# A cross-attention and mixture-of-experts kernel: routing two tiles earlier, first expert tables inside the attention loop, left scatters in threes

## The chip, the cores and the metric

The kernel runs on one NeuronCore of a Trainium2 chip. The metric is the device time of one execution in microseconds (us). Work is split over five engines that run their own instruction streams and meet at semaphores: PE (TensorE: matmuls and transposes; PEld is its weight load), DVE (VectorE), ACT (ScalarE), POOL (GpSimd, which also issues the row scatters) and SP (SyncE, which issues most other transfers).

## The reference, cut to what matters

Input is x of 4 sequences x 1024 tokens x 256, and a context of 77 rows per sequence. All is float32.

```
h   = layernorm(x)
s   = (h Wq + bq)(ctx Wk + bk)^T            # 16 heads of 64, 77 keys each
o   = softmax(s) (ctx Wv + bv) Wo + bo
x1  = x + gamma * norm(h + o) + beta        # norm: layernorm over 256, eps 1e-3
f   = layernorm(x1)
p   = softmax(f Wg)                         # 32 experts
w, i = top_k(p, 4)
y   = sum over k of  w[k] * swiglu(f; W1[i[k]], W3[i[k]], W2[i[k]])     # H = 128
z   = swiglu(f; Ws1, Ws3, Ws2)              # shared FFN, H = 256
out = x1 + y + z
```

Each expert takes at most CAP (2048) pairs of a token and an expert. With 4096 tokens and four experts each, there are 16384 pairs, which is 128 full tiles of 128 rows and some more for the unfilled ends.

## The kernel before

The tokens are cut into 8 blocks of 512 (`NB`), and each block into 4 tiles of 128 tokens (`NC`), so that there are 32 tiles `t`; `blk` is t // 4 and `c` is t % 4. y is block 6 and z is block 7. A block's rows live in `y0[blk]` all through.

**Preparation** multiplies the weights into per-sequence matrices `mq` (scores straight from h) and `vo` (output straight from the probabilities).

**The attention loop** runs over the 32 tiles. In a tile: three groups of heads (6, 5, 5) of `scores` on PE, each with its row maximum `mx` on DVE (L438); `soften`, 16 exponentials on ACT with their sums (L446); `invert`, the reciprocal of the sums on DVE (L456); `divide`, three multiplications on POOL (L461). One tile later PE turns the probabilities (`turn_p`, L479), DVE copies the first part of the result and ACT the rest (L484, L487, L488), PE makes `po` (`output`, L497), and DVE adds it and takes its mean and variance (`residual`, L505 and L355, L356).

Around this, the loop carries steps of other blocks, chosen by `c`:

- for the next block: `measure_in` (DVE statistics), `scale_in` (POOL), `norm_in` (a DVE shift, then four ACT passes, L365), `turn_in` (PE, two ACT copies, L412), `bias_in` (POOL), `keep` (DVE, y = x + beta, L403, in four pieces);
- for block `ffn` = blk - 1: `measure_out` (POOL), `settle` (DVE: two operations L523 and L526, then statistics, in four pieces), `measure_ffn` (POOL), `norm_ffn` (a DVE shift, four ACT passes);
- for block `old` = blk - 2: `turn_ffn` (PE, two ACT copies, L553), `gate` (PE), `turn_gate` (an ACT copy and a PE transpose), `chances` (DVE), `powers` (ACT), `choose` (DVE, top 4 and weights), `mark` (DVE, one-hot of the choices and running counts, L619, L626, L630), `count` (PE), `place` (DVE and POOL, the row number of each pair), and `send`: 16 scatters of 128 rows each, one indirect transfer on POOL's queue (L674), which write each token's row into the buffer `xr` in DRAM, sorted by expert.

**The bridge** follows: it ends block z's normalisation, routes y and z, runs the shared FFN of y and z (`shared_in`, `shared_mid`, `shared_out`: PE ph L704 and pz L730, ACT sg L713, DVE hT), and makes the tables "a": for the first 64 expert tiles, which rows of `xr` they read and which expert they belong to. They come from the counts of blocks 0 to 5. It also issues the last expert weights on SP.

**The expert loop** runs over tiles `j`, four steps deep. SP fetches eight tiles at a time (g, 8 x 136 KB, through row numbers in registers); PE turns g (pgT, copied to gT by DVE, L1080), makes peh (L1086), turns h, makes py (L1107); DVE scales it (L1111); POOL scatters the result rows to `ys` (L1112). Scatters to `xr` that are still open when the loop starts, called left here, are sent one per three tiles; tables "z" for the other tiles are made in its first steps. A switch runs as many of the remaining tiles as the counts ask for.

**The tail** gathers four result rows per token, adds them, and runs the shared FFN of blocks 1 to 5 beside it.

All four are written inside `as_written()`, which pins the order of the instructions on each engine to the order of the code. The order on an engine is thus read directly from the order of the calls.

Of the kernel before, what the change touches and what calls it, by code (L numbers as in the profile page):

```python
# [16 lines left out]
P = 128  # L17
NE = 32
# [12 lines left out]
def kernel(  # L31
# [73 lines left out]
    iota_j = const.tile([P, NJ], F32, name="iota_j")  # L105
    nc.gpsimd.iota(iota_j, [[1, NJ]], base=0, channel_multiplier=0, allow_small_or_imprecise_dtypes=True)
# [260 lines left out]
    def means(name):  # L367
        return sm.tile([P, NC, 2], F32, tag="mv", name=f"mv_{name}", bufs=6)
# [300 lines left out]
    def send(blk, i0, i1):  # L669

        row, xn = rows[blk], xns[blk]
        for i in range(i0, i1):
# [12 lines left out]
            if blk < BA:  # L685
                early.append(sct.ins)
            else:

                tc.declare_no_dep(sct.ins, group="firsts", reason="distinct rows")
                tc.add_to_no_dep_group("lates", sct.ins)  # L690

# [56 lines left out]
    measure_in(0)  # L748
    scale_in(0)
    norm_in(0)  # L750
    turn_in(0)
    bias_in(0)
    keep(0, 0, NC)
    xts[1] = load(1)
    with as_written():
        for t in range(NT):
            blk, c = t // NC, t % NC
            ffn, old = blk - 1, blk - 2
            ahead = blk + 1 < NB
            if c == 0 and blk + 2 < NB:  # L760
                xts[blk + 2] = load(blk + 2)
            if t == 0:

                nc.sync.dma_start(xr[NE * PLACES :, :], none)
                nc.sync.dma_start(
                    xr[: NE * PLACES, :].rearrange("(e q) r -> q e r", q=PLACES)[:P],
                    none.unsqueeze(1).to_broadcast([P, NE, ROW]),
                )
            if t == 18:
                nc.sync.dma_start(ws13[:, :, 0, :], Ws1.rearrange("(k p) f -> p k f", p=P))  # L770
                nc.sync.dma_start(ws13[:, :, 1, :], Ws3.rearrange("(k p) f -> p k f", p=P))
                nc.sync.dma_start(ws2, Ws2.rearrange("(k p) f -> p k f", p=P))
            if t in parts:
                load_experts(*parts[t])
            if c == 1 and ahead:
                scale_in(blk + 1)
            if c == 1 and ffn >= 0:
                measure_out(ffn, 2, 4)
            if c == 3 and ahead:
                bias_in(blk + 1)  # L780
            if c == 3:
                measure_out(blk, 0, 2)
            if c == 3 and ffn >= 0:
                measure_ffn(ffn)
            if c == 1 and old >= 0:
                gate(old)
            if c == 3 and old >= 0:
                count(old)
            sv = [scores(t, g) for g in range(2)]
            if c == 1 and old >= 0:  # L790
                turn_gate(old)
                chances(old)
            soften(t, 0, sv[0])
            if c == 1 and old >= 0:
                powers(old)
            soften(t, 1, sv[1])
            sv.append(scores(t, 2))
            if t >= 1:
                for i in range(3):
                    turn_p(t - 1, i)  # L800
            soften(t, 2, sv[2])
            if c == 0 and old >= 0:
                turn_ffn(old)
            if c == 2 and ahead:
                turn_in(blk + 1)
            if c == 0 and ahead:
                measure_in(blk + 1)
            if c == 1 and old >= 0:
                choose(old)
            if c == 2 and old >= 0:  # L810
                mark(old)
            if c == 3 and old >= 0:
                place(old)
# [496 lines left out]
```

## Time and profile before

| what | us |
|---|---|
| median of 3 runs (lowest, highest) | 800.23 (798.41, 801.84) |
| the profiled execution | 800.8 |
| its span in the profile | 799.0 |
| attention loop, to the end of the last po | 401.25 |
| first peh of the expert loop | 449.30 |
| start of the gather and the tail, about | 732 |

The granted TensorE clock of the profiled execution was 0.974 in the mean. Over the span PE was busy for 733.9 us (92%), DVE for 527.1 (66%), POOL for 402.9 (50%) and ACT for 334.1 (42%). A row of a timeline or a group gives the engine, the line of the code, the operation and its tiles, then its time; a bracket behind it gives the idle time before it and what ended that. In a chain of waits, "issue" is time in which the engine waited for nothing that the profile shows.

### The profile page before, as it was taken

To read this page: it belongs to the slowest core of one execution; us is meant where nothing else is said; L and a number is where in the kernel's file an instruction comes from. 1 tells how busy PE (TensorE), PEld (TensorE's weight loads), DVE (VectorE), ACT (ScalarE), POOL (GpSimd) and SP (SyncE) were. 2 spreads that over 40 slices of the span, in tenths; PEclk is the share of its full clock that TensorE was granted. 3 is DMA by queue.
4 is the path that set the end of the run, shared out by engine and by line. 5 is a ranking of instruction groups with operands and counts; after the bars stand their busy time and mean duration, and the time that the engine had idled before them with its cause. 6 is when DMAs were issued, how large, how long until landed. Compare 5 with 4: busy or idle time off the path is not lost.

```text
span 799.0 us, 12911 instructions
## 1 busy us (share of the span) xinstructions
PE 733.9 (92%) x3508; PEld 542.2 (68%) x3508; DVE 527.1 (66%) x1455; ACT 334.1 (42%) x1586; POOL 402.9 (50%) x488
## 2 busy tenths in 40 slices
PE   6999999999999999999968578879999999999796
PEld 4775767777777777776735457667888878776454
DVE  1874565778777787767665355545767666473897
ACT  0647667676666677766521112221222222221000
POOL 2003333347777777777886355555555555443000
PEclk9999999999999999999998889999999999999988
DMA  8930000404135221513175244465555545422996
GB/s 269 333 101 1 1 1 1 132 1 141 58 100 185 80 98 57 162 57 115 57 242 169 75 125 136 138 197 165 189 165 162 182 146 160 149 96 90 412 412 246
DMA packets 78867, 111.97 MB, mean 140 GB/s; under 512 B 9995, under 2 KB 63679, under 8 KB 78783
## 3 DMA queue, kind: packets, MB, share of 16 engines
q1 hardware_dynamic: 59519, 66.14, 26.7%
q0 software_dynamic: 13056, 36.72, 12.7%
q10 hardware_dynamic: 6208, 8.17, 2.9%
q8 instruction: 31, 0.51, 0.3%
q14 instruction: 53, 0.43, 0.2%
HBM read 62.36 MB, written 48.64 MB: 139 GB/s over the span
## 4 chain that ended last, share of the span: by engine, by line
PE 72%; DVE 10%; ACT 6%; issue 4%; DMA 4%; POOL 3%; DVEq 0%; ACTq 0%; SPq 0%; POOLq 0%
PE peh L1086 16%; PE po L497 14%; PE sc L430 13%; PE py L1107 7%; ACT p L446 5%; PE pgT L1078 4%; PE ph L704 3%; PE pz L730 3%; PE pp L479 2%; PE phT L1100 2%; PE pvo L262 1%; POOL xr L674 1%; PE pvo L287 1%; PE pm L262 1%; DMA gy<-ys 1%
## 5 line engine op out<-in xcount | busy, mean ns | idle before, releaser
L1112 POOL DMA_INDIRECT ys<-y,place x144 | 138.0, 959 | 130.0 <-DVE y L1111 81.2
L446 ACT ACTIVATE p<-sc,mx 128x77 f32<-128x77 f32 x512 | 159.1, 350 | 93.2 <-DVE mx L438 93.2
L1086 PE MATMUL peh<-we,gT 128*128 x576 | 155.0, 393 | 17.7 <-issue 11.4
L497 PE MATMUL po<-we,pT 128*128 128x256 f32 (+1 forms) x640 | 147.1, 383 | 4.6 <-DVE pT L484 3.3
L674 POOL DMA_INDIRECT xr<-xn,row x128 | 127.6, 997 | 35.6 <-issue 34.6
L461 POOL TENSOR_TENSOR p<-p,su 128x385 f32<-128x385 f32 (+1 forms) x96 | 91.0, 973 | 97.2 <-DVE su L456 76.3
L430 PE MATMUL sc<-we,qT 128*128 128x385 f32 (+1 forms) x384 | 138.9, 509 | 0.9 <-POOL qT L416 0.9
L497 PEld LDWEIGHTS po<-we,pT 128*128 128x128 f32 (+1 forms) x640 | 118.4, 190 | 26.7 <-DVE pT L484 5.4
L1094 ACT ACTIVATE h<-peh 128x128 f32<-128x128 f32 x144 | 40.1, 278 | 217.2 <-PE peh L1086 143.8
L1086 PEld LDWEIGHTS peh<-we,gT 128*128 128x128 f32 x576 | 101.5, 196 | 29.7 <-issue 12.8
L446 ACT ACTIVATION_READ_ACCUMULATOR p<-sc,mx 128x1 f32 x512 | 118.7, 232 | 0.0
L430 PEld LDWEIGHTS sc<-we,qT 128*128 128x128 f32 x384 | 71.1, 189 | 54.3 <-issue 27.7
L1095 DVE TENSOR_TENSOR h<-peh,h 128x128 f32<-128x128 f32 x144 | 41.8, 291 | 84.6 <-ACT h L1094 69.1
L1107 PE MATMUL py<-we,ehT 128*128 x288 | 88.3, 389 | 0.9 <-ACT ehT L1102 0.8
L1111 DVE TENSOR_SCALAR y<-py,own 128x256 f32<-128x256 f32 x144 | 69.5, 483 | 17.2 <-PE py L1107 13.1
L438 DVE TENSOR_REDUCE mx<-sc 128x5 f32<-128x385 f32 (+1 forms) x96 | 54.3, 576 | 33.8 <-PE sc L430 31.3
L1080 DVE COPY gT<-pgT 128x256 f32<-128x256 f32 x144 | 59.8, 415 | 7.4 <-PE pgT L1078 4.8
L1078 PE MATMUL pgT<-ident,g 128*128 128x128 f32 x288 | 55.9, 278 | 1.1 <-issue 0.4
L1107 PEld LDWEIGHTS py<-we,ehT 128*128 128x128 f32 x288 | 44.5, 195 | 12.6 <-ACT ehT L1102 1.7
L1078 PEld LDWEIGHTS pgT<-ident,g 128*128 128x128 f32 x288 | 40.6, 144 | 16.9 <-issue 1.6
L1100 PE MATMUL phT<-ident,h 128*128 128x128 f32 x144 | 40.2, 279 | 8.2 <-DVE h L1095 5.9
L730 PE MATMUL pz<-ws,hT 128*128 128x256 f32 x128 | 35.5, 431 | 11.8 <-DVE hT L719 6.3
(200 smaller groups left out, 927.4 us busy)
## 6 DMA issues: line engine op xcount, KB each, us to landing
g<-xr SPq DMA_DIRECT2D x144, 136.0 KB
gy<-ys SPq DMA_DIRECT2D x16, 1024.0 KB
xr<-y SPq DMA_DIRECT2D x1, 4352.0 KB
y<-in_x SPq DMA_DIRECT2D x8, 512.0 KB
out<-y ACTq DMA_DIRECT2D x16, 256.0 KB
xnd<-xnT SPq DMA_DIRECT2D x6, 512.0 KB
we<-in_W SPq DMA_DIRECT2D x8, 384.0 KB
ys<-y,place POOLq DMA_INDIRECT x144
```

What stands on the lines that cost most here:

```text
L430: nc.tensor.matmul(sc[:, : (h1 - h0) * SK], qTs[blk][:, k, o : o + P], mq[:, b, k, h0 * SK : h1 * SK], start=(k == 0), stop=(k == KC - 1),)
L446: nc.scalar.activation(probs[t][:, h, :], sv[:, h - h0, :], AF.Exp, bias=mx[:, h : h + 1], accum_out=su[:, h : h + 1],)
L461: nc.gpsimd.tensor_tensor(p[:, h0:h1, :], p[:, h0:h1, :], su[:, h0:h1].unsqueeze(2).to_broadcast([P, h1 - h0, SK]), ALU.mult,)
L497: nc.tensor.matmul(po[:, :D], pT[:n, i, :], vo[b][:n, i, :], start=(i == 0), stop=(i == KT - 1))
L674: sct = nc.gpsimd.indirect_dma_start(out=xr, out_offset=bass.IndirectOffsetOnAxis(ap=row[:, i : i + 1], axis=0), in_=xn[:, c, :], in_offse ...
L730: nc.tensor.matmul(pz[:, c * D : (c + 1) * D], hT[:, f, (2 * c2 + c) * P : (2 * c2 + c + 1) * P], ws2[:, f, :], start=(f == 0), stop=(f == ...
L1078: nc.tensor.transpose(pt[:, k * P : (k + 1) * P], g[:, j % RG, k * P : (k + 1) * P], ident)
L1080: nc.vector.tensor_copy(gT.rearrange("p k t -> p (k t)"), pt[:, :D])
L1086: nc.tensor.matmul(ph[:, : 2 * H], gT[:, k, :], we[:, ds(ev[j] * EW + k * 2 * H, 2 * H)], start=(k == 0), stop=(k == KC - 1),)
L1107: nc.tensor.matmul(py[:, :D], hT, we[:, ds(ev[j] * EW + KC * 2 * H, D)], start=True, stop=True)
L1111: nc.vector.tensor_scalar(y, py[:, :D], own[:, i, 1:2], None, ALU.mult)
L1112: sent = nc.gpsimd.indirect_dma_start(out=ys, out_offset=bass.IndirectOffsetOnAxis(ap=place_[:, i : i + 1], axis=0), in_=y, in_offset=None,)
```

## The change

The order of the loop's side steps is rewritten; nearly nothing is added or removed.

- `measure_in` of block blk + 2 is called at c = 2; `scale_in` and `norm_in` of the next block at c = 0, `turn_in` at c = 1, `bias_in` at c = 2 (each one tile earlier than before, from block 1 on).
- For `ffn`: the three pieces of `settle` that were called at c = 0, 1 and 2 are called together at c = 1, behind `invert` and `divide`. `measure_ffn` and `norm_ffn` come at c = 2, `turn_ffn` and `gate` at c = 3 between the calls of `soften`.
- For `old`: `turn_gate`, `chances`, `powers`, `choose` and `mark` all come at c = 0, `mark` behind `invert` and `divide` (before: c = 2, ahead of them). `count` and `place` come at c = 1.
- `keep` runs in one go of four pieces at c = 3.
- Scatters go through a list `left`: four per tile from `place` on, and six in the last two tiles, so that those of block 5 all go in the loop.
- In the last block, y is routed inside the loop: `measure_ffn` and `norm_ffn` at t = 29, `turn_ffn` and `gate` at t = 30, `turn_gate` to `mark` at t = 31; `count` and `place` follow the loop. A second `settle` of z is called at t = 31.
- The tables "a" are made at t = 29 to 31. Their tiles lie in another pool, and their wide scratch in the buffer of `oh`. The table `iota_j` is gone: its values are computed from `behind`, and `e_col` is replaced by one more product.
- In the bridge, the fetches of the first two groups of expert tiles come first on SP, ahead of the last five weight loads. The scatters of y go in lots of three (the last of two), and a lot's first scatter waits for the step just before it.
- In the expert loop the 13 left scatters of z go one per four tiles; before there were 16, one per three tiles. Its first two fetches have moved out.

The diff, cut to its core:

```diff
--- before.py
+++ after.py
...
-    iota_j = const.tile([P, NJ], F32, name="iota_j")
-    nc.gpsimd.iota(iota_j, [[1, NJ]], base=0, channel_multiplier=0, allow_small_or_imprecise_dtypes=True)
...
-            if t in parts:
-                load_experts(*parts[t])
-            if c == 1 and ahead:
-                scale_in(blk + 1)
-            if c == 1 and ffn >= 0:
-                measure_out(ffn, 2, 4)
-            if c == 3 and ahead:
-                bias_in(blk + 1)
-            if c == 3:
-                measure_out(blk, 0, 2)
-            if c == 3 and ffn >= 0:
-                measure_ffn(ffn)
-            if c == 1 and old >= 0:
-                gate(old)
-            if c == 3 and old >= 0:
-                count(old)
-            sv = [scores(t, g) for g in range(2)]
-            if c == 1 and old >= 0:
-                turn_gate(old)
-                chances(old)
-            soften(t, 0, sv[0])
-            if c == 1 and old >= 0:
-                powers(old)
-            soften(t, 1, sv[1])
-            sv.append(scores(t, 2))
-            if t >= 1:
-                for i in range(3):
-                    turn_p(t - 1, i)
-            soften(t, 2, sv[2])
-            if c == 0 and old >= 0:
-                turn_ffn(old)
-            if c == 2 and ahead:
-                turn_in(blk + 1)
-            if c == 0 and ahead:
-                measure_in(blk + 1)
-            if c == 1 and old >= 0:
-                choose(old)
-            if c == 2 and old >= 0:
-                mark(old)
-            if c == 3 and old >= 0:
-                place(old)
-            invert(t)
-            divide(t)
-            if c == 1 and ahead:
-                norm_in(blk + 1)
-            if c == 3 and ffn >= 0:
-                norm_ffn(ffn)
-            if c == 3:
-                settle(blk, 0)
-            elif ffn >= 0:
-                settle(ffn, c + 1)
-            if c >= 2 and ahead:
-                keep(blk + 1, 2 * c - 4, 2 * c - 2)
-            if t >= 11:
-                b11, c11 = divmod(t - 11, NC)
-                send(b11, c11 * TOPK, (c11 + 1) * TOPK)
-            if t >= 1:
-                residual(t - 1, output(t - 1))
...
-        del left[:4]
-        measure_out(z, 2, 3)
-        settle(z, 1)
-        sends(3)
-        turn_ffn(y)
-        for i in range(3):
-            turn_p(NT - 1, i)
-        settle(z, 2)
-        residual(NT - 1, output(NT - 1))
-        measure_out(z, 3, 4)
-        gate(y)
-        turn_gate(y)
-        chances(y)
-        powers(y)
-        settle(z, 3)
-        sends(2)
-        measure_ffn(z)
...
-        if first:
-            nc.vector.tensor_scalar(e_col, ones[:NE, :], iota_p[:NE, :], None, ALU.mult)
...
-        oj, t1, t2 = wide("oj"), wide("t1"), wide("t2")
-        nc.vector.tensor_scalar(oj, iota_j[:NE, :n], start, None, ALU.is_ge)
-        nc.vector.tensor_scalar(t1, iota_j[:NE, :n], end, None, ALU.is_ge)
+        if first:
+            room = lt2.tile([P, NK, NE], F32, tag="oh", name="room").rearrange("p n e -> p (n e)")
+            oj, t1, t2, t3 = (room[:NE, i * NA : (i + 1) * NA] for i in range(4))
+        else:
+            oj, t1, t2, t3 = wide("oj"), wide("t1"), wide("t2"), wide("t3")
+        nc.vector.tensor_scalar(t3, behind[:NE, :n], behind[:NE, 0:1], 1.0 / P, ALU.subtract, ALU.mult)
+        nc.vector.tensor_scalar(oj, t3, start, None, ALU.is_ge)
+        nc.vector.tensor_scalar(t1, t3, end, None, ALU.is_ge)
         nc.vector.tensor_tensor(oj, oj, t1, ALU.subtract)
-        nc.vector.tensor_scalar(t2, iota_j[:NE, :n], base, float(P), ALU.subtract, ALU.mult)
+        nc.vector.tensor_scalar(t2, t3, base, float(P), ALU.subtract, ALU.mult)
         if not first:
             nc.vector.tensor_copy(t1, t2)
             nc.vector.tensor_scalar(t2, t2, most, None, ALU.min)
             nc.vector.tensor_tensor(t1, t1, t2, ALU.subtract)
             nc.vector.tensor_tensor(t1, t1, oj, ALU.mult)
         nc.vector.scalar_tensor_tensor(t2, t2, first_e, oj, ALU.add, ALU.mult)
+        nc.vector.tensor_scalar(t3, oj, iota_p[:NE, :], None, ALU.mult)
...
-        nc.tensor.matmul(p_e[:, :n], e_col, oj, start=True, stop=True)
+        nc.tensor.matmul(p_e[:, :n], ones[:NE, :], t3, start=True, stop=True)
...
-        for part in range(5):
-            load_experts(*parts[NT + 1 + part])
-        ta = tables("a", msum_a, NA)
-        choose(y)
-        shared_in(y, 0, AF.Tanh)
-        norm_ffn(z)
-        mark(y)
-        sends(7)
-        shared_mid(y, 0)
-        next(ta)
-        shared_in(y, 1, AF.Tanh)
-        turn_ffn(z)
         count(y)
-        gate(z)
-        next(ta)
         place(y)
-        assert not left
         left += [(y, i) for i in range(NK)]
-        turn_gate(z)
-        chances(z)
-        powers(z)
-        next(ta)
-        shared_mid(y, 1)
-        shared_out(y)
-        next(ta)
-        choose(z)
-        shared_in(z, 0, AF.Silu)
-        mark(z)
-        count(z)
-        msum_z = sm.tile([P, NE], F32, tag="msum_z", name="msum_z", bufs=1)
-        nc.vector.tensor_copy(msum_z, cums[NB][:, 0, :])
-        tz = tables("z", msum_z, NJ - NA)
-        sends(5)
-        shared_mid(z, 0)
-        place(z)
-        left += [(z, i) for i in range(NK)]
-        shared_in(z, 1, AF.Silu)
-        shared_add(y)
-        shared_mid(z, 1)
-        sends(11)
-        shared_out(z)
-        shared_add(z)
...
+    left = []
+    def sends(n, after=None):
+        for i, (blk, k) in enumerate(left[:n]):
+            sct = send(blk, k, k + 1)
+            if after is not None and i == 0:
+                tc.add_manual_dep(sct, after, SYNC, reason="rows in small lots")
+        del left[:n]
+    def last():
+        return nc.cur_bb.bb.instructions[-1].name
+        for t in range(NT):
+            blk, c = t // NC, t % NC
+            ffn, old = blk - 1, blk - 2
+            ahead, end = blk + 1 < NB, blk == z
+            if t == 0:
+                measure_in(1)
+            if t in parts:
+                load_experts(*parts[t])
+            if c == (t < NC) and ahead:
+                scale_in(blk + 1)
+            if c == 1 and ffn >= 0:
+                measure_out(ffn, 2, 4)
+            if c == 2 + (t < NC) and ahead:
+                bias_in(blk + 1)
+            if c == 3:
+                measure_out(blk, 0, 2)
+            if c == 2 and ffn >= 0 and not end:
+                measure_ffn(ffn)
+            sv = [scores(t, g) for g in range(2)]
+            if c == 1 and old >= 0:
+                count(old)
+            if c == 0 and old >= 0:
+                turn_gate(old)
+                chances(old)
+            if c == 3 and end:
+                turn_gate(y)
+                chances(y)
+            soften(t, 0, sv[0])
+            if c == 0 and old >= 0:
+                powers(old)
+            if c == 3 and end:
+                powers(y)
+            soften(t, 1, sv[1])
+            if c == 3 - end and ffn >= 0:
+                turn_ffn(ffn)
+            sv.append(scores(t, 2))
+            if t >= 1:
+                for i in range(3):
+                    turn_p(t - 1, i)
+            if c == 3 - end and ffn >= 0:
+                gate(ffn)
+            if t >= NT - 2:
+                next(ta)
+            soften(t, 2, sv[2])
+            if c == 1 + (t < NC) and ahead:
+                turn_in(blk + 1)
+            if c == 0 and old >= 0:
+                choose(old)
+            if c == 1 and old >= 0:
+                place(old)
+                left += [(old, i) for i in range(NK)]
+            if c == 2 and blk + 2 < NB:
+                measure_in(blk + 2)
+            if c == 3 and end:
+                choose(y)
+            invert(t)
+            divide(t)
+            if c == 0 and old >= 0:
+                mark(old)
+            if c == 3 and end:
+                mark(y)
+            if c == (t < NC) and ahead:
+                norm_in(blk + 1)
+            if c == 1 and ffn >= 0:
+                for i in range(1, NC):
+                    settle(ffn, i)
+                if end:
+                    measure_ffn(ffn)
+            if c == 2 - end and ffn >= 0:
+                norm_ffn(ffn)
+            if c == 3:
+                settle(blk, 0)
+                if end:
+                    settle(blk, 1)
+                else:
+                    keep(blk + 1, 0, NC)
+            sends(6 if t >= NT - 2 else TOPK)
+            if t >= 1:
+                residual(t - 1, output(t - 1))
+            if t == NT - 3:
+                ta = tables("a", cums[BA][:, 0, :], NA)
+            if t >= NT - 3 and t < NT - 1:
+                next(ta)
+        assert not left
+        measure_out(z, 2, 3)
         count(y)
+        for i in range(3):
+            turn_p(NT - 1, i)
         place(y)
         left += [(y, i) for i in range(NK)]
+        settle(z, 2)
+        sends(3)
+        residual(NT - 1, output(NT - 1))
+        measure_out(z, 3, 4)
+        sends(2)
...
+    with as_written():
+        fetch(0)
+        fetch(RG)
+        for part in range(5):
+            load_experts(*parts[NT + 1 + part])
+        shared_in(y, 0, AF.Tanh)
+        settle(z, 3)
+        measure_ffn(z)
+        shared_in(y, 1, AF.Tanh)
+        shared_mid(y, 0)
+        norm_ffn(z)
+        sends(3, last())
+        shared_mid(y, 1)
+        turn_ffn(z)
+        sends(3, last())
+        shared_out(y)
+        gate(z)
+        turn_gate(z)
+        chances(z)
+        powers(z)
+        shared_in(z, 0, AF.Silu)
+        choose(z)
+        sends(3, last())
+        mark(z)
+        count(z)
+        msum_z = sm.tile([P, NE], F32, tag="msum_z", name="msum_z", bufs=1)
+        nc.vector.tensor_copy(msum_z, cums[NB][:, 0, :])
+        tz = tables("z", msum_z, NJ - NA)
+        shared_in(z, 1, AF.Silu)
+        sends(2, last())
+        shared_mid(z, 0)
+        place(z)
+        assert not left
+        left += [(z, i) for i in range(NK)]
+        shared_mid(z, 1)
+        sends(3)
+        shared_out(z)
+        shared_add(y)
+        shared_add(z)
...
-        fetch(0)
         for j in range(NM_ + len(steps)):
-            if j % RG == 1 and j + RG - 1 <= NM_:
+            if j % RG == 1 and RG < j + RG - 1 <= NM_:
                 fetch(j + RG - 1)
             if j in (4 * RG + 4, 5 * RG + 4, 6 * RG + 4):
                 fetch_shared(j // RG - 4, nc.sync)
                 jj = j - i
                 if 0 <= jj < NM_:
                     made[jj, i + 1] = step(jj, made.pop((jj, i), None))
-            if j % 3 == 0:
+            if j % 4 == 0:
                 sends(1)
             if j in (2, 5, 8, 11):
                 next(tz)
```

## The prediction

> **What bounds the kernel now.** I read the page's table of slices first: PE is at 9 tenths or more in all slices but those from about 400 to 560 us and the ends. So there are four stages: attention loop to 401 us, bridge to 449, experts to 732, tail. The page does not say what paces the loop, because PE and a second chain are equally full there. The chain of waits over tiles 4 and 5, early in the loop, where PE carries little of the chain yet, shows the second one whole (start, us, what):
>
> ```profile
> 101.06 3.48 ACT p L446 x22
> 104.54 0.47 ACT pT L484
> 105.30 1.53 ACT p L446 x10
> 106.86 0.25 DVE su L456
> 107.11 0.32 DVE qb L523
> 107.46 1.08 DVE y L526
> 108.56 0.44 DVE st L355
> 109.02 0.18 DVE mv L356
> 109.20 0.32 DVE qb L505
> 109.54 0.44 DVE st L355
> 110.19 0.53 DVE mx L438
> 110.80 3.48 ACT p L446 x22
> ```
>
> One cycle per tile: row maximum, the exponentials on ACT, the reciprocal (`invert`), then whatever DVE has been given after `invert`, then the next tile's maximum. DVE works in program order, so each us put after `invert` lengthens the cycle, and each us between maximum and `invert` is free, since DVE waits there for ACT. In the settled blocks the first `mx` of tiles 16 to 20 start at 226.83, 236.76, 246.89, 257.87, 269.28: cycles of 9.93, 10.13, 10.98, 11.41, sum 42.4. From `mx` to `invert` is 6.44 to 6.57 us in each, 6.79 where the routing's small ACT operations fall. PE's own work per block of four tiles is 4 x (4.14 scores + 1.09 transposes + 4.32 output) and 2.9 for the block's other products: 41.1. Chain and PE are balanced; there is 1.3 us of slack.
>
> What DVE does when is in its timeline for tiles 17 and 18; of it, the operations that matter:
>
> ```profile
> 250.51 0.68 DVE L619 TENSOR_TENSOR oh<-iota_e,idx 128x512 f32<-128x512 f32 x1
> 251.22 1.05 DVE L626 TENSOR_REDUCE mask<-oh 128x128 f32<-128x512 f32 x1
> 252.31 0.87 DVE L630 TENSOR_TENSOR cum<-cum,mask 128x32 f32<-128x32 f32 x4
> 253.33 0.25 DVE L456 RECIPROCAL su<-su 128x16 f32<-128x16 f32 x1 [0.15 <-ACT p L446]
> 255.58 1.36 DVE L403 TENSOR_TENSOR y<-y,beta_b 128x256 f32<-128x256 f32 x2
> ```
>
> `mark` (first three lines, 2.6 us) stands ahead of the reciprocal: hidden. `settle` (2.08 from L523 to L356), two pieces of `keep` (1.28) and `residual` (1.0) stand behind it.
>
> The bridge's chain ends so, PE having finished its work at 441:
>
> ```profile
> 440.63 0.44 PE pgT L1078 x4
> 441.06 8.23 issue
> 449.30 2.05 PE peh L1086 x4
> ```
>
> PE's products of 440.6 are taken by DVE only at 448.2, while 16 row fetches (429 to 446) and twelve scatters share the queues. In the expert loop the copies `gT` of the first 48 tiles span 448.78 to 556.36, 107.6 us; settled tiles take 1.63, which would be 78.2. The loss of 29.4 ends with the last left scatter, at 554.7:
>
> ```profile
> 540.00:550.00 10.00, 8.06 (x38) 6.07 (x38) 5.08 (x17) 1.75 (x8) 6.44 (x7) 0.93 0.54 183
> 560.00:570.00 10.00, 9.84 (x54) 8.32 (x55) 6.89 (x23) 2.60 (x12) 6.56 (x7) 1.00 0.54 170
> ```
>
> (us, PE, PEld, DVE, ACT, POOL busy, clock, DMA share, GB/s.) Same DMA load, but PE at 8.06 against 9.84.
>
> **The change part by part.** *Loop, settled blocks.* The total work is the same; what counts is which side of `invert` it lands on.
> c=0: `mark` moves behind `invert`. Its L619 has two SBUF inputs, and POOL divides there. The row nearest is L526: 0.48 to 0.64 with POOL idle, 1.03 in the mean beside the divides; I add 0.6 to L619. Reciprocal 0.17 + mark 3.2 + shift 0.1, then ACT's four `norm_in` (2.1, L365) before the next exponentials, which would otherwise start 0.7 after `mx`: cycle 6.79 + 0.17 + 3.2 + 0.1 + 2.1 − 0.7 = 11.7.
> c=1: three `settle` in a row: 0.17 + 2.08 + 1.9 + 1.5 (only the first two overlap divides) + residual 1.0 = 6.65; with 6.5: 13.15.
> c=2: only shift and residual follow `invert`, so DVE would allow 7.8. PE does not: DVE's pT copy ends 2.4 after `mx`, ACT's at 5.0, po ends at 7.2, the next scores' first group at 8.8. Cycle 8.9: the time won here is cut off by PE.
> c=3: `turn_ffn`'s two xnT copies (1.1, L553) now stand between the exponentials; before they followed them. 7.6 + 0.17 + settle 2.08 + keep of four (1.28, then 0.7 with POOL free) + residual 1.0 = 12.8.
> Sum 46.55 against 42.3: +4.25 per block, five blocks (2 to 6): +21.3. Block 1 has no `mark`: 43.65 against 41.9, +1.8.
> `choose` (2.3) and `place` (1.7) stay ahead of `invert`, hidden under ACT's 6.5; `measure_in` (2.2) likewise, at c=2. POOL still sends four rows per tile (1.27 each from the starts of L674) after three divides (2.9): 8.0 of 10 or more, no bound. SP issues the same loads in the loop.
> *Last block.* t=28: mark alone, +1.4. t=29: `norm_ffn(6)`'s shift stands on DVE before the residual and waits for POOL's `measure_ffn` (0.3 + 1.05, L350), itself behind the third settle: 5.65 + 1.35 + residual 1.1 + four small table steps 0.7 gives a cycle near 15.4 against 10.1, +5.3; POOL's four sends wait behind it too, and end before the next divides. t=30: −0.4. t=31: mark, two settles and residual precede DVE's copy of pT(31), and so po(31): +3. Sum +9.3.
> Loop: 21.3 + 1.8 + 9.3 = **+32**, so po(31) ends at 433 instead of 401. Bounds +22 (copies and marks uncontended, PE floor lower) to +40 (PE gap of 4 us in t=30 or 31 halves its clock, which it did in 418.9 to 425.7, behind an idle of 5.1 us).
> *Bridge.* Before: 401.3 to 449.3, 48. After, from po(31)'s end: residual 1.0; POOL's last `measure_out`, behind three sends, 5.8; settle 7.0; measure_ffn behind two sends 9.7; ACT norm 12; pxn and xnT 15; PE's shared_out(y) (16 pz, 4.9) and gate 20; powers with a table load (1.28) 22.5; choose 25; mark 27.5; count 28.5; shared_in(z,1) 3.65 and its hT 33.5; eight pz 36; first peh about 36. The tables and both fetches are issued near its start on SP, ahead of the 3 MB of weights, and nothing waits for them; the 8.2 stall and the table wait go. The scatters in threes wait for steps that POOL does not need; the queue is 16 x 1.27 = 20 us, within 36. **−12**; −4 if the stall returns with the scatters in a later place, −15 at best.
> *Experts.* 13 left scatters instead of 16, every fourth tile, and two of the fetches gone. Nothing in the trace shows the loss per scatter at this spacing: by proportion 29.4 x 3/16 = −5.5, and the first eight tiles' excess (15.9 against 13.0) −2.5: **−8**. Bounds 0 and −29.
> Here a rule speaks against any gain. The rows show PE's results seen late as long as scatters and fetches mix. The Trainium skill, "SBUF — State Buffer", section "SBUF: two separate sides", says that engine ports and DMA ports are disjoint, so that a DMA cannot slow a compute operation. By the rule fewer overlapped scatters free no engine, the term is 0, and the sum 820; by the row −8, and 812. I take the row, since the lag ends in the tile of the last scatter.
> *Small edits.* `iota_j` out, one more table operation: 0.2 us, once, in the loop's last tiles. The tail's code is the same: 0.
> Sum against the profiled execution (800.8 us, span 799.0): 800.8 + 32 − 12 − 8 = 812.8. The median of the runs is 800.2, 0.6 lower: **812**.
>
> **The rivals.** *Likeliest, 0.62:* as above, 803 to 822.
> *The lag in the experts goes altogether (0.15).* POOL's scatters per tile fall from 1.27 x 4/3 = 1.69, over the tile's 1.63, to 1.27 x 5/4 = 1.59, under it. If the lag is a POOL queue that never empties, the first 48 tiles return to 1.63: 32 − 12 − 29 = −9, 791. Above a return of 24 of the 29 us the kernel is faster. Against it: 1.69 over 1.63 explains 3 us in 48 tiles, not 29, and single lags of 1 to 7 us follow fetches.
> *The loop is not lengthened in the middle (0.10).* If DVE catches up in c=2, blocks stay at 42.3 and only the last block pays: +9 − 12 − 8, 790 to 797. Against it: cycles of 9.93 to 11.4 repeat to 0.2 us over five blocks, so no slack is carried.
> *The loop is lengthened more (0.13).* PE's clock drops in the new gaps and the stall in the bridge stays: 40 − 4 − 3, up to 833.
>
> **How the numbers follow.** Half a per cent, 4 us, is about what a measurement of this kernel can tell from no change. Of the likeliest, some 0.05 lies below 804; the second gives 0.11 faster and 0.04 same; the third 0.07 faster and 0.03 same; the last is slower. Together, with rounding, faster 0.17, same 0.12, slower 0.71. The range 796 to 827 leaves out most of the second and third cases' fast ends and the extreme of the last; the likeliest's own is 803 to 822.
>
> **What would show it.** First `mx` of a settled block: cycles near 11.7, 13.2, 8.9, 12.8 and a block near 46.5; PE about 41 of it. po(31) ending near 433; first peh some 36 later with no long issue before it; 48 gT in about 100 us. I am wrong if the block stays under 44, or if the expert tiles run at 1.63 from the start.

## The result, and the profile after

The changed kernel takes 825.55 us in the median of four runs (823.36 to 826.49), against 800.75 for the kernel before beside it: a ratio of 1.031, 95% interval 1.028 to 1.034. It is 24.8 us slower. The forecast had the side and its cause, but only 12 of the 24.8; the time lies at the upper end of its range, 796 to 827. One later execution of the changed kernel took 1525.6 us at a granted clock of 1.00, which nothing here explains, and is left out. The profiled execution of the changed kernel has a span of 824.6, 25.6 over the 799.0 of before. In the table, each stage as the traces have it, beside the forecast:

| stage | before | forecast | after | moved by (forecast) |
|---|---|---|---|---|
| end of po(31) | 401.3 | 433 | 449.4 | +48.1 (+32) |
| from there to the first peh | 48.05 | 36 | 33.4 | −14.7 (−12) |
| 48 gT of the expert loop | 107.6 | 99.6 | 99.6 | −8.0 (−8) |
| from gT 48 to the end | 242.6 | 242.6 | 242.8 | +0.2 (0) |

So it is mainly the loop's term that was mis-sized. Each tile's cycle, from its first `mx` (row maximum) to the next tile's, by c, in the settled blocks (2 to 6):

| | c = 0 | c = 1 | c = 2 | c = 3 | block |
|---|---|---|---|---|---|
| before | 9.93 | 10.13 | 10.98 | 11.28 | 42.3 |
| forecast | 11.7 | 13.15 | 8.9 | 12.8 | 46.55 |
| after | 11.40 | 13.70 | 10.11 | 12.74 | 47.95 |

The chain of waits of the changed kernel at the turn from c = 1 to c = 2 (start, us, what) shows where the c = 2 cycle went:

```profile
313.77 0.32 DVE qb L503
314.11 0.44 DVE st L353
314.76 1.47 DVE mx L436 x3
316.22 0.73 issue
316.95 6.24 PE po L495 x20
323.20 1.57 PE sc L428 x4
324.79 0.65 DVE mx L436
```

Twenty matmuls of po take 6.24 us here. At the same turn of the kernel before they follow PE's other work without an idle, and take 4.49:

```profile
293.65 4.49 PE L497 MATMUL po<-we,pT 128*128 128x256 f32 x20
```

The turn of the changed kernel in PE's timeline, and in a table of stretches (us, busy time of PE, PEld, DVE, ACT and POOL, granted clock, DMA share, GB/s):

```profile
312.98 1.25 PE L477 MATMUL pp<-ident,p 128*128 128x128 f32 x10
316.95 6.24 PE L495 MATMUL po<-we,pT 128*128 128x256 f32 x20 [2.72 <-DVE mx L436]
```

```profile
314.00:317.00 3.00, 0.28 (x4) 0.08 (x1) 2.93 (x8) 1.62 (x11) 2.44 (x3) 1.00 0.31 98
317.00:319.00 2.00, 2.00 (x5) 1.57 (x6) 1.80 (x8) 2.00 (x14) 1.29 (x2) 0.54 0.21 70
319.00:321.00 2.00, 2.00 (x7) 1.67 (x6) 0.00 (x0) 2.00 (x13) 0.00 (x0) 0.60 0.00 0
321.00:323.00 2.00, 2.00 (x11) 1.76 (x10) 0.27 (x2) 1.66 (x6) 1.42 (x2) 1.00 0.00 0
```

PE stands idle for 2.72 us, because DVE's three settles hold up the copy of pT that po waits for, and then its clock is halved for 3.4 us (by the two middle rows: 2 x 0.46 / 0.5 + 2 x 0.40 / 0.5). It is so at the same place in all five settled blocks. The three settles themselves, in DVE's timeline for c = 1:

```profile
307.84 0.25 DVE L454 RECIPROCAL su<-su 128x16 f32<-128x16 f32 x1 [3.11 <-ACT p L444]
308.44 1.06 DVE L524 SCALAR_TENSOR_TENSOR y<-qb,rs,y 128x256 f32<-128x256 f32 x1
310.66 0.86 DVE L524 SCALAR_TENSOR_TENSOR y<-qb,rs,y 128x256 f32<-128x256 f32 x1
312.61 0.48 DVE L524 SCALAR_TENSOR_TENSOR y<-qb,rs,y 128x256 f32<-128x256 f32 x1
313.69 0.39 DVE L503 TENSOR_TENSOR qb<-po,qb 128x256 f32<-128x256 f32 x1
```

1.06, 0.86, 0.48: POOL's three divides run from 308.2 to 311.2, so the first two of these stand beside them and the third behind, as the forecast had it.

In the last tiles, again from the chain of waits, the shift at t = 29 behind POOL, and po(31) at t = 31:

```profile
409.39 0.25 POOL ve L346
409.71 1.06 POOL rs L348
410.79 0.17 DVE sh L359
410.99 2.08 ACT xn L363 x4
413.12 1.33 PE pxn L550 x5
414.45 2.21 PE sc L428 x4
```

```profile
442.77 6.60 PE L495 MATMUL po<-we,pT 128*128 128x256 f32 x20 [2.09 <-DVE pT L482]
```

PE idles 4.08 us before the first pxn (at 411.6), and its clock is 0.50 in 414 to 416. Before po(31) it idles for 2.83 and 1.06 us while `mark` holds DVE, then for 2.09 more behind the settles, and the clock is 0.50 from 440 to 446, so that po takes 6.6. Ahead of `mark`, DVE also waits for two products of the tables (DVE's timeline at t = 31):

```profile
430.17 0.21 DVE L818 TENSOR_SCALAR r_tab_a<-p_r_a 1x64 int32<-1x64 f32 x1 [1.74 <-PE p_e_a L816]
431.60 0.23 DVE L820 COPY e_all_a<-p_e_a 128x64 f32<-128x64 f32 x1 [1.22 <-remote]
```

"remote" marks a wait whose end the profile can't put down to an instruction. In the bridge, the answer to the line "441.06 8.23 issue" of before is:

```profile
463.13 3.32 issue
481.59 0.44 PE pgT L1098 x4
482.03 0.72 issue
482.75 1.10 PE peh L1106 x4
```

The stall before the first peh is gone. One of 3.3 us has come earlier: the product lg ends at 463.1, and ACT takes it at 466.1.

### The profile page after: what moved, and what is told of

It reads as the page before. It is cut to its first block, busy times and chain, and to the rows that moved or that the text cites. A ratio compares the mean times of both kernels' runs of the same rounds, so it can differ in the third digit from the quotient of the medians.

```text
span 824.6 us, 12909 instructions
## 1 busy us (share of the span) xinstructions
PE 744.1 (90%) x3508; PEld 548.7 (67%) x3508; DVE 521.0 (63%) x1457; ACT 333.6 (40%) x1586; POOL 402.2 (49%) x487
## 3 DMA queue, kind: packets, MB, share of 16 engines
q1 hardware_dynamic: 59519, 66.14, 25.6%
## 4 chain that ended last, share of the span: by engine, by line
PE 51%; DVE 21%; ACT 14%; issue 5%; DMA 4%; POOL 3%; another core or an unknown queue 1%; DVEq 0%; ACTq 0%; SPq 0%; POOLq 0%
PE peh L1106 15%; ACT p L444 10%; PE po L495 10%; PE py L1127 7%; PE sc L428 6%; PE pgT L1098 4%; DVE y L524 2%; DVE mx L436 2%; DVE gy L1223 2%; DVE st L353 2%; PE phT L1120 2%; ACT qb L363 2%; DVE cum L628 1%; DVE y L1224 1%; PE ph L703 1%
## 5 line engine op out<-in xcount | busy, mean ns | idle before, releaser
L495 PE MATMUL po<-we,pT 128*128 128x256 f32 (+1 forms) x640 | 158.5, 404 | 20.4 <-DVE mx L436 13.6
L1106 PE MATMUL peh<-we,gT 128*128 x576 | 151.0, 385 | 10.6 <-DVE gT L1100 4.8
L495 PEld LDWEIGHTS po<-we,pT 128*128 128x128 f32 (+1 forms) x640 | 125.6, 201 | 46.8 <-issue 20.3
L672 POOL DMA_INDIRECT xr<-xn,row x128 | 128.2, 1001 | 43.7 <-issue 34.3
L459 POOL TENSOR_TENSOR p<-p,su 128x385 f32<-128x385 f32 (+1 forms) x96 | 89.0, 953 | 122.8 <-DVE su L454 76.1
L428 PE MATMUL sc<-we,qT 128*128 128x385 f32 (+1 forms) x384 | 141.6, 511 | 0.9 <-POOL qT L414 0.9
L1106 PEld LDWEIGHTS peh<-we,gT 128*128 128x128 f32 x576 | 98.8, 191 | 21.9 <-DVE gT L1100 6.2
L1115 DVE TENSOR_TENSOR h<-peh,h 128x128 f32<-128x128 f32 x144 | 41.8, 291 | 79.1 <-ACT h L1114 65.7
L1131 DVE TENSOR_SCALAR y<-py,own 128x256 f32<-128x256 f32 x144 | 69.4, 482 | 16.5 <-PE py L1127 11.8
L436 DVE TENSOR_REDUCE mx<-sc 128x5 f32<-128x385 f32 (+1 forms) x96 | 52.3, 574 | 30.0 <-PE sc L428 21.5
L454 DVE RECIPROCAL su<-su 128x16 f32<-128x16 f32 x32 | 8.1, 253 | 77.5 <-ACT p L444 77.5
```

Of the source, the lines that this page charges most:

```text
L428: nc.tensor.matmul(sc[:, : (h1 - h0) * SK], qTs[blk][:, k, o : o + P], mq[:, b, k, h0 * SK : h1 * SK], start=(k == 0), stop=(k == KC - 1),)
L436: nc.vector.tensor_reduce(mx[:, h0:h1], sv, AX.X, ALU.max, negate=True)
L459: nc.gpsimd.tensor_tensor(p[:, h0:h1, :], p[:, h0:h1, :], su[:, h0:h1].unsqueeze(2).to_broadcast([P, h1 - h0, SK]), ALU.mult,)
L495: nc.tensor.matmul(po[:, :D], pT[:n, i, :], vo[b][:n, i, :], start=(i == 0), stop=(i == KT - 1))
L672: sct = nc.gpsimd.indirect_dma_start(out=xr, out_offset=bass.IndirectOffsetOnAxis(ap=row[:, i : i + 1], axis=0), in_=xn[:, c, :], in_offse ...
L1106: nc.tensor.matmul(ph[:, : 2 * H], gT[:, k, :], we[:, ds(ev[j] * EW + k * 2 * H, 2 * H)], start=(k == 0), stop=(k == KC - 1),)
```

## The experiments

The first four ran where the kernel before takes 759.0 us (757.8 to 760.7) and not 800. The ratios are to the kernel before on the same chip, and the cycles of the settled blocks can be compared directly: those that an edit does not touch are the same to 0.1 us there. The expected times were worked out from 825 and don't hold here.

**1. The clock alone.**

```diff
-                    turn_p(t - 1, i)
+                    turn_p(t - 1, i, 2 if c == 2 and blk >= 2 and not end else 1)
...
-        for c in cs:
+        for c in [c for _ in range(times) for c in cs]:
```

> The changed kernel, but the transposes of p are issued twice in the tiles with c = 2 of blocks 2 to 6 (1.25 us more PE work per block, same result). Theory (clock): in these tiles PE stood idle for 2.7 us before po, and its clock then halved (matmuls of 634 ns instead of 379). With the gap filled to 1.5 us the matmuls stay at 379, po takes 4.5 instead of 6.2, the c = 2 cycle falls from 10.1 to 8.9, five blocks give -6: about 819. Rival (PE's order, not its clock, sets that cycle): more PE work gives 0 to +1.3 per block, 825 to 832.

The c = 2 cycle is 9.16 instead of 10.11 (8.9 expected), and a block 47.0 instead of 47.95; c = 0, 1 and 3 are unchanged. 795.8 us, ratio 1.048 (1.046 to 1.051). PE's timeline at the same turn of block 4:

```profile
262.30 2.35 PE L477 MATMUL pp<-ident,p 128*128 128x128 f32 x20
266.27 1.97 PE L495 MATMUL po<-we,pT 128*128 128x256 f32 x8 [1.62 <-DVE pT L482]
268.70 2.86 PE L495 MATMUL po<-we,pT 128*128 128x256 f32 x12 [0.47 <-ACT pT L482]
```

More PE work makes the tile shorter. After an idle of 1.62 us nearly all matmuls take 379 ns, and none takes the 634 of the changed kernel; the clock in 267 to 271 is 1.00. So 0.95 us per block, 4.8 in the loop, was the halved clock. The changed kernel did not run on this chip, so the gain in total time was not measured.

**2. mark ahead of invert.**

```diff
+            if c == 0 and old >= 0:
+                mark(old)
             invert(t)
             divide(t)
-            if c == 0 and old >= 0:
-                mark(old)
```

> The changed kernel with mark at c = 0 put back ahead of invert (blocks 2 to 7). Theory (what stands behind invert lengthens the tile's cycle): choose ends 4.9 after mx and mark takes 2.7, so invert comes 0.9 later, but 2.8 behind it goes: the c = 0 cycle falls from 11.4 to 9.3 or 9.9 (where PE begins to bind), six times: 813 to 816. Rival (the sum of DVE's work counts, not its place): no change, 825.

c = 0 takes 9.35 (9.3 expected). c = 2 falls to 9.16 too: PE's idle there is 1.15 us with the settles still behind `invert`, and the clock stays. c = 1 falls from 13.70 to 13.38. A block is 44.62. 782.5 us, ratio 1.030 (1.027 to 1.032): 13.3 below experiment 1 on the same chip. Where DVE's work stands decides, not its sum.

**3. The three settles ahead of invert.**

```diff
+            if c == 1 and ffn >= 0:
+                for i in range(1, NC):
+                    settle(ffn, i)
+                if end:
+                    measure_ffn(ffn)
             invert(t)
             divide(t)
```

(and away from behind it)

> The changed kernel with the three settles of c = 1 ahead of invert instead of behind it. Theory: they fill DVE's wait for ACT; place ends 4.3 after mx, three settles at 1.5 end at 8.9, so the c = 1 cycle is 10.0 instead of 13.7; the gap of PE that halved its clock in c = 2 goes too, 8.9 instead of 10.1. Block 43 instead of 47.95; blocks 1 to 6 and t = 29: about 793. Rival (only the settles' total counts): 825. Rival (PE's clock alone is the cause): -6, 819.

c = 1 takes 9.62 (10.0 expected), and no idle of PE over 1 us is left in the settled blocks. But c = 2 takes 10.7 and not 8.9, since PE, busy without a longer idle, is now behind, and c = 3 takes 13.06: a block is 44.8, not 43. 778.5 us, ratio 1.025 (1.023 to 1.028).

**4. settle and keep ahead of invert in all tiles.**

```diff
+            if c == 3:
+                settle(blk, 0)
+                if end:
+                    settle(blk, 1)
+                else:
+                    keep(blk + 1, 0, NC)
             invert(t)
             divide(t)
```

(with experiment 3's edit, and away from behind)

> As e3_settle_ahead, and at c = 3 settle and the four keeps are ahead of invert as well; mark stays behind it. Theory: behind invert there is little left but mark and residual, DVE's and ACT's cycles sum to some 37 per block, and PE's 41.1 of work sets the block: 41.5 instead of 47.95, po(31) ends near 404, and with the bridge and the experts of the changed kernel about 779. Rival (DVE's total work or POOL is the limit): a block stays above 44, 795 or more.

A block takes 44.5, not 41.5: the rival's figure. 778.0 us, ratio 1.025 (1.022 to 1.028), no more than experiment 3. (That it meets the 779 expected is chance: the kernel before is 41 us quicker on this chip.) DVE's timeline says why; POOL's small steps stand behind its four sends:

```profile
260.72 0.93 DVE L359 SCALAR_TENSOR_TENSOR sh<-mv,rs 128x4 f32<-128x4 f32 x1 [2.14 <-POOL rs L348]
269.43 0.49 DVE L524 SCALAR_TENSOR_TENSOR y<-qb,rs,y 128x256 f32<-128x256 f32 x1 [1.97 <-POOL rs L513]
```

What stands ahead of `invert` is free only if its inputs are there.

**5 and 6. The two kernels once more, unchanged.**

> The kernel before, unchanged, once more for its trace beside the next three: the experiments of the first call ran where it takes 759 and not 800. Theory (transfers): its attention loop is the same 42.3 per block, po(31) ends near 401, and what is missing lies in the bridge (the 8.2 stall) and in the first 48 expert tiles (29 us of late results), which run at 1.63 per tile. Rival: every stage is shorter in proportion.

> The changed kernel, unchanged, on the same chip as r_before. Theory: the loop is as long as in its first profile (47.95 per block, po(31) ends near 448), since nothing of it hangs on transfers; the gain in the expert tiles, 8 us in the first profiles, is absent where there are no late results, and the bridge is shorter by some 7 instead of 14.7. So it loses more: near 801 where the kernel before takes 759. Rival (the gains belong to the new order of scatters and fetches): 759 + 25 = 784.

This time the chip was again one with 800: 799.6 (ratio 0.999, 0.998 to 1.000) and 827.4 us (ratio 1.035, 1.033 to 1.037). So the question of where the chip of experiments 1 to 4 is quicker could not be answered for the kernel before. The two runs repeat the stages: po(31) ends at 400.4 and 448.3, the bridge takes 48.4 and 34.3, 48 gT take 107.1 and 99.9. For the changed kernel the traces of experiments 1 to 4 answer it. There the bridge takes 31.4 to 31.5 in the first three (35.0 in the fourth), ACT takes the product lg as soon as it ends (439.13 after 439.10 in experiment 3), and from gT 16 on every eight tiles up to the 56th take 13.0, with the same 13 left scatters among them. On the chips with 800 those groups take 14.4 to 19.0 in the changed kernel. So late results come with the chip as much as with the program.

**7. Before, with settle and keep ahead of invert.**

```diff
+            if c == 3:
+                settle(blk, 0)
+            elif ffn >= 0:
+                settle(ffn, c + 1)
+            if c >= 2 and ahead:
+                keep(blk + 1, 2 * c - 4, 2 * c - 2)
             invert(t)
             divide(t)
```

(and away from behind)

> The kernel before with settle and keep ahead of invert instead of behind it, nothing else. Theory (what stands behind invert sets the cycle until PE binds): 42.3 per block falls to PE's own 41.1 or a little over, 7 blocks: -5 to -8. At c = 3 settle waits for POOL's measure_out behind four sends, which may take back 1 to 2 per block: then 0. Rival (place makes no difference): 0 in every cycle.

798.8 us, ratio 0.999 (0.997 to 1.001), and a block of 42.13 against 42.33; 5 to 8 us less were expected, or 0. The chain of waits over a block is PE's but for one turn over DVE of 1.2 us, and PE is busy for 41.8 of the 42.13, not for the 41.1 of the forecast's sum. The kernel before was at PE's limit already, with next to nothing to gain.

**8. As 4, with mark ahead, and the sends behind POOL's small steps.**

```diff
+            if c == 0 and old >= 0:
+                mark(old)
             invert(t)
             divide(t)
...
             if c == 2 and ffn >= 0 and not end:
                 measure_ffn(ffn)
+            if t <= NT - 3:
+                sends(TOPK)
...
+            if t >= NT - 3:
-            sends(6 if t >= NT - 2 else TOPK)
+                sends(6 if t >= NT - 2 else TOPK)
```

> As e4_all_ahead, with mark ahead of invert at c = 0 too, and the four sends of a tile behind POOL's measure steps of the next tile instead of ahead of them. Theory: c = 0 falls from 11.4 to 9.9, c = 2 from 10.7 to 9.9 and c = 3 from 12.1 to 10.5, as the waits for rs (2.1 and 2.0) go; a block takes 41.5 instead of 44.5, PE sets it, and the time is 15 to 20 below e4_all_ahead. Rival (POOL's sends then hold up its divides): block 43 or more.

Cycles of 10.1, 11.7, 9.3 and 11.8, a block of 42.76 (41.5 expected). 796.0 us, ratio 0.995 (0.993 to 0.997): with the loop nearly back at PE's limit, the rest of the change is a small gain on such a chip. Against the first profile of before, the loop's end is 14.5 later, the bridge 8.9 shorter (39.1) and the 48 gT 9.4 (98.2). po(31) ends at 415.7, since from t = 29's `mx` to there it still takes 13.5 more than before.

**9. One part alone: before, with tables and fetches early.**

```diff
         ta = tables("a", msum_a, NA)
+        for _ in range(4):
+            next(ta)
         choose(y)
...
         sends(7)
+        fetch(0)
+        fetch(RG)
         shared_mid(y, 0)
```

(the four later steps, `iota_j`, `e_col` and the loop's own first two fetches taken out as in the change)

> The kernel before with one part of the change alone: the tables a in one go at the start of the bridge, without iota_j and e_col, and the first two fetches issued behind the seven sends, as soon as block 5's scatters have landed (some 416 instead of 429). Loop, sends and expert loop are those of before. Theory (the bridge's gain comes from fetching earlier): the 8.2 stall before the first peh goes, the bridge takes 38 to 42 instead of 48, the time is 6 to 10 lower. Rival (the stall follows the fetches, wherever they are): a hand-over in the middle of the bridge waits as long, and the gain is 0 to 3.

799.7 us, ratio 1.000 (0.999 to 1.002). The fetches go out at 419.8 instead of 429.2, and the bridge takes 47.7 (48.05 and 48.4 in the two profiles of before). The stall has split up (chain of waits):

```profile
436.82 2.75 another core or an unknown queue
445.64 2.71 issue
```

The rival is right: the earlier fetch is worth nothing by itself. That leaves y's routing, which has left the bridge, as what shortens it; this was not run alone.

**10. As 8, with the last tiles and c = 1 relieved.**

```diff
-                for i in range(1, NC):
+                for i in range(2, NC):
                     settle(ffn, i)
...
-            if c == 3:
+            if c == 3 and not end:
                 settle(blk, 0)
+                settle(blk, 1)
+                keep(blk + 1, 0, NC)
...
+            if c == 2 and end:
+                norm_ffn(ffn)
             soften(t, 1, sv[1])
...
+        mark(y)
+        settle(z, 0)
+        settle(z, 1)
+        po = output(NT - 1)
+        count(y)
```

(mark of y and the two settles of z taken out of t = 31, norm_ffn of y out of t = 29; place and the sends of y behind the last residual)

> e7_all_and_mark with three more moves: the second settle of a block at c = 3 too (two instead of three at c = 1); norm_ffn of y in t = 30 behind its first exponentials, where its shift waits for nothing; mark of y and two settles of z behind DVE's copy of pT(31) instead of ahead of it. Theory (DVE's order sets loop and end): c = 1 falls from 11.7 to 10.2, a block from 42.75 to 41.5, t = 29 to 31 lose 10 together; po(31) ends near 400 instead of 415.7, and the time is 10 to 14 below e7_all_and_mark. Rival (work moved out of the last tiles comes back in the bridge): 2 to 4 below.

796.3 us, ratio 0.995 (0.994 to 0.997): nothing below experiment 8. po(31) ends at 410.6, 5 earlier and not 16, and the bridge takes 43.5 instead of 39.1. The block stays at 42.75, though c = 1 fell from 11.7 to 10.9: PE is busy for 42.1 of it, so hardly anything is left to win. The rival is right about the bridge, where what left the loop comes back (chain of waits):

```profile
417.36 1.20 POOL xr L672
421.39 3.90 DMA xr<-xn,row
425.29 0.61 ACT xn L363
425.94 0.48 PE pxn L550
429.37 8.69 another core or an unknown queue
```

In both kernels z's normalisation waits for a small step of POOL behind five scatters of y, and these start only once y's `place` is done, which now follows the last residual. The step ends at 425.1 here and at 425.7 in experiment 8, so the earlier end of the loop is lost: PE idles for 8.0 us before that pxn, against 4.0. The last line is not what has changed. It holds PE's shared FFN, and ACT takes the product lg 4.1 us after its end; in experiment 8 that is 3.9.

**11. The changed kernel with no scatter left for the expert loop.**

```diff
         shared_mid(z, 1)
-        sends(3)
+        sends(NK)
         shared_out(z)
```

> The changed kernel, but all 16 scatters of z are sent in the bridge; none is left for the expert loop. Theory (late results come where row scatters and row fetches mix): the first 48 tiles take 82 to 88 instead of 99.6, against up to 8 us at their start, where POOL is still sending: 5 to 15 below the changed kernel on this chip. Rival (the fetches or the result scatters alone cause it): the tiles stay near 100 and the time is the same or higher. Where a chip shows no late results, 0 to +8.

821.9 us, ratio 1.025 (1.020 to 1.029), against 1.031 (1.028 to 1.034) and 1.035 (1.033 to 1.037) of the changed kernel on like chips; the first two intervals touch. The first eight tiles take 27.2 and the next 18.0, and then nearly every eight take 13.02. The first 48 take 97.3, since the start costs 14 and not up to 8; the first 72 take 136.7 instead of 140.9 and 141.7. The same stretch of the changed kernel, and of this one:

```profile
530.00:545.00 15.00, 11.92 (x63) 9.34 (x62) 7.42 (x25) 3.17 (x14) 8.16 (x9) 1.00 0.42 138
```

```profile
530.00:545.00 15.00, 15.00 (x85) 12.62 (x84) 10.59 (x34) 3.90 (x18) 8.91 (x10) 1.00 0.56 179
```

PE is full with more transfers beside it, not fewer. On these chips the late results belong to the stretch where left row scatters and row fetches mix.

**12. Experiments 10 and 11 together.**

> e10_best with all 16 scatters of z sent in the bridge, as in e11_none_left. Theory (the two gains are in different stages and add up): on a chip with late results 796.3 - 5.6 = 790 to 792, against some 800 of the kernel before; the first eight tiles take 25 to 28, tiles 16 to 63 run at 13.0 per eight. Rival (the bridge of e10_best, whose hand-overs are late already, gets longer when POOL sends more in it): 796 or more. On a chip without late results the sends only cost: some 760.

792.5 us, ratio 0.991 (0.989 to 0.993): 7.3 below the kernel before on its chip, and the best of all; 790 to 792 was expected. Its bridge takes 43.4, as in experiment 10, its first eight tiles 27.1, and its gT 16 to 56 run at 13.02 per eight. The first 72 tiles take 136.5 instead of the 141.8 of experiment 10.

## Why the forecast was right in kind and wrong in size

- **The mechanism held.** What stands behind `invert` lengthens the tile. c = 0 and c = 3 came within 0.3 of their working, and experiments 2 and 3 undid one piece each and found its own cycle to 0.4 us (the next one, c = 2 of experiment 3, was 1.8 off).
- **The step that failed first: "po ends at 7.2, the next scores' first group at 8.8. Cycle 8.9".** It took PE at full clock. The forecast had noted that DVE holds up pT, but did not ask how long PE then stands: 2.72 us, after which its clock halves. The cycle is 10.11. Over five blocks this step is 1.2 x 5 = 6.0 short, of which experiment 1 shows 0.95 x 5 = 4.8 to be the clock.
- **c = 1** was 0.55 short: ACT's four `norm_in` of c = 0 still hold back the next tile's exponentials there (0.3 by experiment 2, where they come earlier), and the settles took some 0.2 more. c = 0 was 0.3 long. All settled blocks together: 1.4 x 5 = 7.0 short.
- **Blocks 0 and 1**: 1.5 short, and the loop began 0.2 later. The four keeps in one go at c = 3 were costed at nothing in block 0, where that cycle took 11.83 instead of 11.15.
- **The step that failed as badly, the last block: "t=30: −0.4" and "t=31: +3".** t = 30 took 13.05 instead of 10.0, since the scores' third group stands behind pxn, which waits for `norm_ffn` of t = 29 and then runs at half clock. From t = 31's `mx` to the end of po(31) it is 23.9 instead of 19.9. What the forecast had put at +3, from `invert` to the copy of pT(31), took 2.8 more than before. It had left out 2.0 of halved po, and 2.1 by which `invert` came later, behind the two table products that DVE took late. In experiment 1 DVE waits for neither product, and the stretch takes 21.4: this part goes with the chip. With t = 29's +0.3 the last block is 7.3 short. The halved clock of these tiles stood in the bound (+40) and in the fourth rival, not in the sum; its share there was read in the trace and not tested.
- 7.0 + 1.5 + 0.2 + 7.3 = 16.0, the whole distance from +32 to +48.1. The fourth rival came nearest, but it kept the stall in the bridge, and its +40 was still 8 short.
- **The slack of 1.3 us** that the forecast saw between DVE's chain and PE was next to nothing: PE is busy for 42.0 of the 42.3 us of a block, not for 41.1 (experiment 7).
- **The bridge** was right to 3 us, but only in part for the reason given: the fetches' place is worth nothing alone (experiment 9).
- **The experts** came to the forecast's −8.0 (−7.1 in experiments 5 and 6), which is in part luck, as the basis is only half right. Experiment 11 confirms that the left scatters carry the loss, but experiments 1 to 4 show 13 of them without it. The step that weighed the rule of the Trainium skill ("SBUF — State Buffer", "SBUF: two separate sides") is not contradicted: PE ran full at a DMA share of 0.56 in experiment 11, and what is late are hand-overs.
- **Contended operations**: L617 was given 0.6 for POOL's divides and took 0.63, as it had ahead of `invert` (0.68). It starts 0.2 us before the first divide. Of the four small adds L628, the two beside the divides took 0.53 and 0.75 and the two behind them 0.19 each, as all four did before: +0.9. The sum of `mark` was right by two errors.

What stays open is what delays the hand-overs, and why on some chips only. The trace's own record of semaphore events narrows it: the receiving engine starts within 0.03 us of PE's event, and it is this event that is late. In the changed kernel lg ends at 463.13 and its event comes at 466.11. In the kernel before three products end between 440.63 and 441.06, and their events come together, from 448.15 to 448.24. As the ends of matmuls are modelled, this does not tell whether PE itself was late or only its event.

## What to carry to other kernels

Where two engines hand a tile to and fro, ask of each moved step on which side of the wait it lands. Ahead of the wait it is free while its inputs are there; behind it, it is paid in full. Before a cycle is called bound by PE, work out how long PE will idle in the new order: here 1.6 us was harmless, and 2.7 us cost half the clock for 3.4 us. A kernel that stands at PE's limit gains nothing from a shorter chain beside it, and loses at once when the chain gets longer.

## What the runs showed of the hardware

- PE's clock halved after each of five idles of 2.71 to 2.72 us, and stayed after seven of 1.58 to 1.63 (changed kernel and experiment 1). The Trainium skill, "TensorE: Matmul & The Clock Gate", section "Part 1: The HAM clock gate", gives an idle window of some 3.4 us; here less was enough.
- The clock records of all fourteen traces say more. In each, the slow-downs start on a fixed grid of 3.41 us and last whole steps of it, but for the last, which the end of the kernel cuts short. Between 60 and 760 us, every step at full clock in which PE was busy for under 0.42 of the time was followed by half clock, none over 0.61 was, and between the two both occur. So where an idle falls on the grid counts too: the five idles of 2.7 us recur every 47.95 us, close to 14 steps (47.79), and fall at nearly the same place.
- The kernel before takes 759.0 us on one chip and 800 on others. The chips with 800 show results of PE taken some 1 to 8 us late in the bridge and in the first 56 to 72 expert tiles; the traces of the other do not show it in gT 16 to 56.
- With all 16 scatters of z sent in one go, 13 of them in the first 16 us of the expert loop, the first eight tiles took 27.2 us instead of 12.9 and 13.4, and the whole was still 3.7 and 5.5 us below the two medians of the changed kernel.
